# Sums of products in a Mamba block: accumulating DMAs in place of transposes and a vector add, under a new instruction order

## The chip, the cores and the metric

The kernel runs on one core of one Trainium2 chip. The time is the device time of one execution in microseconds; the time of a kernel is the median of its runs. The core has a matrix engine (TensorE, "PE" in the profile; its weight loads are "PEld"), a vector engine (VectorE, DVE), an activation engine (ScalarE, ACT), GpSimd (POOL), a queue engine that mostly issues transfers (SyncE, SP), and 16 DMA engines that all queues share.

## The reference, cut to what matters

One sequence of 4096 positions with 1024 features goes through half an FFN step, a Mamba block and another half FFN step, each behind a layer norm without weights:

```python
x = x + 0.5 * ffn(layernorm(x))      # weights rounded to -1, 0, 1 times a scale
x = x + mamba(layernorm(x))
x = x + 0.5 * ffn(layernorm(x))

# mamba
u, z = split(x @ W_in.T)             # 1024 features each
u = silu(conv(u, 4 taps) + conv_b)
dt_r, B, C = split(u @ W_xproj.T)    # 64, 16, 16
dt = softplus(dt_r @ W_dt.T + b_dt)
h_t = exp(dt * A) * h_(t-1) + dt * B_t * u_t      # 16 states for each feature
y_t = sum over the 16 states of h_t * C_t, + u * Dskip
out = (y * silu(z)) @ W_out.T
```

The sum over the states is what the change deals with: for every feature and position there are 17 terms, 16 products `h * C` and the skip `u * Dskip`.

## The kernel before, in words

All arithmetic is float32; the FFN splits its input in a high and a low part, so that two fast matmuls do for one.

**Tiling.** The sequence is cut into 16 chunks (`c`) of 256 positions, and the 1024 features of the Mamba block into two halves (`half`) of four blocks of 128 features. A half of a chunk is a tile of 128 partitions (features) by 4 x 256 elements, 512 KB. The recurrence runs over 32 halves, and in each over 16 states `n`.

**The recurrence of a state.** SP fetches rows B and C of the state, broadcast over the partitions (`bc`, six buffers, `fetch`). POOL writes `h = g * B` (line 934, `g = u * dt`) and adds what comes over from the chunk before to the first column (line 944); there are three `h` buffers. ACT makes the decays `da` (line 911) into PSUM. DVE scans `h` along the positions (line 969, two scans a state) and multiplies by C into a product `p` (line 985); there are five `p` buffers. ACT saves the last column (line 952) and the buffer of `h` comes free.

**The sum over the terms.** A term that is summed alone goes to PE: eight transposes of 128 x 128 (line 1052, `summed`) add it in PSUM to `y`, which also turns it from features by positions to positions by features. To save transposes, some pairs of terms are added first. Three states of each half (`SENT`: 1, 5 and 9) are sums by DMA: POOL issues an accumulating DMA that adds product `n - 1` onto product `n` within SBUF (line 1020, `beside`). One state of a middle chunk's half (`PAIRED`: 7), two of a half in the first chunk (12 and 14) and none in the last chunk are added by DVE (line 1002, `paired`). So a half in the middle has 13 terms left for PE out of 17. DVE then multiplies `y` by `silu(z)` (line 1069, `gate`), PE turns the result back (line 743) and multiplies by W_out (line 751).

**Around the recurrence**, the chunk before and the chunk after are worked on at the same time: statistics and norm (lines 382 to 401), transposes (417), the FFN (488, its residual on DVE in line 468), the projections to `u` (608) and `z` (668), convolution (539 on ACT, 549 on DVE). Weights stream from HBM through five buffers (lines 353, 360 and 366, issued by SP, loaded two or three blocks ahead). The FFN's bias is added to `x` by an accumulating DMA of POOL (line 461).

**What sets the order.** The program is written out by a planner that runs when the kernel is built (`Streams`). Every part is a generator that asks for an engine with a duration and an earliest time; the planner gives the engine to whichever can start first, by rank where several can, and holds an engine back for a better rank within `HOLD`. The constants at the top are its reckoning: `ISSUE` and `ADDED` for an accumulating DMA (600 and 9500 ns), `LATE_*` for what it adds to the end of an operation, ranks such as `SUM` and `RECUR`, and `TRIG`, which says after which step of the recurrence each part of the neighbouring chunks may start. The order that comes out is fixed on each engine: an instruction waits in its engine's queue, and what stands behind it waits too. The planner's times decide only this order; on the chip, semaphores do.

Of the kernel before, what the change touches and what calls it, by code (L numbers as in the profile page):

```python
# [27 lines left out]

FULL, PASS, TURN = 0.844, 0.449, 0.855
REACH = 160  # L30
ISSUE, ADDED = 600, 9500
SWITCH = 1300

LATE_P, LATE_X, LATE_D, LATE_N = 400, 100, 1700, 1300
PAIRED = (7,)
PAIRED_FIRST = (12, 14)
PAIRED_LAST = ()
TRIG = (-11, -16, 5, 1, -6, -16, 16, -2, 9, 12, 0, -17, 7, -7, -19, -8, -12)
ENTERED = 2
POOLED = ()  # L40
SENT = (1, 5, 9)
DEFER = 2.2, 3.2
Q_SOON = False

DECAY, ENTER, SUM, PREPARE, RECUR, GATE = 5, 0, 0, 0, 4, 1
FFN_A, NORM, U_PART, CONV, DELTA, OUT, FFN_C = 0, 5, 1, 3, 4, 2, 1

HOLD = (1300, 0, 100, 2600)
Z = (5, 7)


class Streams:
# [109 lines left out]
def macaron_mamba_kernel(  # L162
# [169 lines left out]

    def streamed(load, n, ahead, rank):

        queue = []

        def fill():
            for i in range(n):
                yield lambda: 0 if len(queue) < ahead else INF
                w = yield from weights.take()  # L340
                load(i, w)
                queue.append((order.now + 5000, w))

        order.spawn(fill(), rank)
        return queue

    def arrived(queue):
        yield lambda: queue[0][0] if queue else INF
        return queue.pop(0)[1]

    def u_weights(i, w):
# [76 lines left out]
            order.spawn(parts(g, pt, end + REACH), rank)  # L428


    def ffn(c, which, rank, at, tiles=range(TT)):
        ln, rows_, at = yield from stats(c, at, tiles)
        key = which, c

        def split(t):

            xn, begin = yield from normed(c, ln, rows_, t, at)
            hi = yield from his.take()
            lo = yield from los.take()
            ends = []  # L440

            def cut(g, pt, at_):
                part_hi, part_lo = (flat(p_[:, 4 * g : 4 * g + 4, :]) for p_ in (hi, lo))
                end = yield act(512, at_)
                nc.scalar.copy(part_hi, pt)  # L445
                end = yield dve(600, end + REACH)
                nc.vector.tensor_tensor(part_lo, pt, part_hi, ALU.subtract)  # L447
                banks.put(pt, end)
                ends.append(end)
                if len(ends) == NB // 4:  # L450
                    ready["parts", key, t] = end + REACH + LATE_N
                    parts[t] = lo, hi

            order.spawn(biased(t, begin), rank)
            yield from transposed(xn, begin, cut, rank)

        def biased(t, at_):

            yield from when("hbias")
            end = yield pool(ISSUE, at_, False)  # L460
            nc.gpsimd.dma_start(x_tiles[c, t], hbias.to_broadcast([P, D]), accum_op=ALU.add)
            ready["bias", key, t] = end + ADDED

        def residual(t, cols, pf, at_):
            at_ = max(at_, (yield from when("bias", key, t)))
            end = yield dve(660, at_)
            xt = x_tiles[c, t][:, cols]
            nc.vector.scalar_tensor_tensor(xt, pf, hscl, xt, ALU.mult, ALU.add)  # L468
            (ys if (*key, t) == ("a", 0, 1) else banks).put(pf, end)
            ready["ffn", key, t, cols.start] = end  # L470
            if key == ("c", NC - 1):
                yield from give_out(c, t, cols, end)

        parts = {}
        for t in tiles:
            order.spawn(split(t), rank)
        if key == ("a", 0):
            yield from as_weights_come(key, parts, residual, rank)
        for t in tiles if key != ("a", 0) else ():
            begin = yield from when("parts", key, t)  # L480
            lo, hi = parts[t]
            for h in range(2):
                cols = slice(h * OH, (h + 1) * OH)
                pf = yield from banks.take()
                for x in (lo, hi):
                    end = yield pe(8 * OH * PASS, 0, "r")
                    for k in range(NB):
                        nc.tensor.matmul(  # L488
                            pf,
                            x[:, k, :],  # L490
                            wf[:, k, cols],
                            start=(x is lo and k == 0),
                            stop=(x is hi and k == NB - 1),
                        )
                order.spawn(residual(t, cols, pf, end + REACH + LATE_X), rank)
            los.put(lo, end)
            his.put(hi, end)
        lns.put(ln, end if key != ("a", 0) else order.now)
        ends = {}
        for t in tiles:  # L500
            left = yield from when("ffn", key, t, 0)
            right = yield from when("ffn", key, t, OH)
            ends[t] = max(left, right)
        return ends

    def as_weights_come(key, parts, residual, rank):

        for t in range(TT):
            yield from when("parts", key, t)
        groups = {}  # L510
        for h in range(2):
            groups[0, h] = yield from banks.take()
            groups[1, h] = yield from ys.take()
        for k in range(NB):
            yield from when("wf", k)
            end = yield pe(8 * OH * PASS, 0, "r")
            for (t, h), pf in groups.items():
                for i in range(2):
                    nc.tensor.matmul(
                        pf,  # L520
                        parts[t][i][:, k, :],
                        wf[:, k, h * OH : (h + 1) * OH],
                        start=(k == 0 and i == 0),
                        stop=(k == NB - 1 and i == 1),
                    )
        for (t, h), pf in groups.items():
            order.spawn(residual(t, slice(h * OH, (h + 1) * OH), pf, end + REACH), rank)
        for t in range(TT):
            los.put(parts[t][0], end)
            his.put(parts[t][1], end)  # L530
# [4 lines left out]
    def conv(c, blk, pp, at):  # L535
        half, b = divmod(blk, HB)
        ub, rows_ = u[c, half][:, b, :], pp[:, KER - 1 : KER - 1 + T]
        end = yield act(T, at)
        nc.scalar.activation(  # L539
            ub,  # L540
            rows_,
            AF.Identity,
            bias=pr[:, blk, C_CB : C_CB + 1],
            scale=pr[:, blk, C_CW + KER - 1 : C_CW + KER],
        )
        for k in range(KER - 1):
            end = yield dve(391, end + (REACH if k == 0 else 111))
            tap = pr[:, blk, C_CW + k : C_CW + k + 1]
            nc.vector.scalar_tensor_tensor(ub, pp[:, k : k + T], tap, ub, ALU.mult, ALU.add)  # L549
        banks.put(pp, end)  # L550
        done = ready.setdefault(("conv", c, half), [])
        done.append(end)
        if len(done) == HB:
            end = yield act(D, end + REACH, "silu")
            nc.scalar.activation(flat(u[c, half]), flat(u[c, half]), AF.Silu)
            ready["u", c, half] = end + REACH

    def front():
        for c in range(NC):
# [28 lines left out]
            for t in range(TT):  # L588
                xn, at = xns[t]
                yield from transposed(xn, at, keep, NORM)  # L590
                while len(ends) < 2 * (t + 1):
                    yield lambda: ends[2 * t + 1] if len(ends) > 2 * t + 1 else INF

            end = yield pool(190)
            nc.gpsimd.tensor_copy(xT[:, :, PAD - KER + 1 : PAD], halo)  # L595
            at = max(end, ends[-1]) + REACH
            yield U_PART
            for blk in range(NB):
                yield from step(c, 2 + blk // 2)
                if blk % HB == 0:  # L600
                    u[c, blk // HB] = yield from us.take()
                pp = yield from banks.take()
                w = yield from arrived(queue)
                wt = w.rearrange("p (k m) -> p k m", m=P)
# [75 lines left out]
    def kept(c, half, b, pp, at):  # L680
        end = yield act(512, at)
        nc.scalar.copy(sz[c, half][:, :, b * P : (b + 2) * P], pp)
        banks.put(flat(pp), end)
        if b + 2 == HB:
            z = flat(sz[c, half])
            end = yield act(D, end + 125, "silu")
            nc.scalar.activation(z, z, AF.Silu)
            ready["z", c, half] = end + REACH

# [37 lines left out]
    def turned(c, half, yT):  # L727
# [15 lines left out]
                nc.tensor.transpose(pt[:, cols], sz[c, half][:, t, cols], ident)  # L743
            order.spawn(keep(t, pt, end + REACH), OUT)
        szs.put(sz[c, half], end)
        yield lambda: ends[-1] if len(ends) == TT else INF

    def by_w_out(po, yT, w, half, t):
        wt = w.rearrange("p (k m) -> p k m", m=QW)
# [207 lines left out]
    def recur():  # L957
        behind = None
        for c, half, n in items:
# [4 lines left out]
            for j in range(2):  # L964
# [3 lines left out]
                rows_ = flat(h[:, 2 * j : 2 * j + 2, :])  # L968
                nc.vector.tensor_tensor_scan(rows_, flat(da), rows_, 0.0, ALU.mult, ALU.add)  # L969
                decays.put(da, end)  # L970
                ready["step", (2 * c + half) * NST + n] = end
                if behind and j == 0:
                    yield from left(*behind)
                if behind and j == (0 if Q_SOON else 1):
# [38 lines left out]
    def beside(c, half, n):  # L1013
# [4 lines left out]
        if n in SENT:  # L1018
            end = yield pool(ISSUE, at, False)
            nc.gpsimd.dma_start(flat(p), flat(q), accum_op=ALU.add)  # L1020
            end = end + ADDED
        else:
            for j in range(0, HB, 2):
                end = yield pool(1250, at, True)
# [128 lines left out]
```

## Time and profile before

| | |
|---|---|
| median of 3 runs | 2602.99 us (2601.02 to 2603.2) |
| the profiled execution | 2601.62 us, span from first to last instruction 2599.9 us |
| busy PE, DVE, ACT, POOL | 2441.9, 2314.4, 1925.1, 1896.4 us |
| transposes of the sum on PE (line 1052) | 3328, 438.5 us |
| adds of pairs on DVE (line 1002) | 32, 53.7 us |
| sums by DMA (line 1020) | 96, issue 85.5 us on POOL in all |
| bytes moved by DMA | 461.03 MB, 177 GB/s |

In the rows of the profile, `L934` is line 934 of the kernel, `out<-in` the tiles that an instruction writes and reads, `x1024` how many there are; then come the busy time in all, the mean duration of one, the idle time of the engine just before, and what ended most of it. fp32 matmuls stand as two instructions each. "`A <- B`: total, times, longest" in the waits means that A stood still until B was done. The DMA share is the mean busy share of the 16 DMA engines.

### The profile page before, as it was taken

What the parts mean: (1) busy time and instruction counts of PE and PEld (TensorE: products, weight loads), DVE (VectorE), ACT (ScalarE), POOL (GpSimd) and SP (SyncE); (2) the same over time, 40 slices, a digit from 0 to 9 for tenths busy, and PEclk for the clock granted to TensorE, in tenths of its full rate; (3) what the DMA queues carried; (4) which work ended last, traced back from release to release, by engine and by line L of the source; (5) the groups of instructions that cost most, each with busy time, mean ns of one, the idle gap of its engine ahead of it and who ended that gap; (6) DMA issues with size and microseconds to landing.
All of it is one profiled execution on the core that took longest, in us unless ns stands there. A gap on an engine that the chain in (4) does not pass through costs nothing. (4 is left out here: it accounts for less than half of the span.)

```text
span 2599.9 us, 39031 instructions
## 1 busy us (share of the span) xinstructions
PE 2441.9 (94%) x13058; PEld 2093.8 (81%) x13058; DVE 2314.4 (89%) x2468; ACT 1925.1 (74%) x4056; POOL 1896.4 (73%) x2041
## 2 busy tenths in 40 slices
PE   5988899999999999999999999999999999999787
PEld 4776787888888888888888888888888888887676
DVE  4588998999999899999989999899999989999795
ACT  3678677687877868787786868878687786877563
POOL 0467867778787787878778686877878677787683
PEclk9989999999999999999999999999999999999888
DMA  4546556766766666666566765665675567666462
GB/s 165 156 129 187 175 158 178 198 180 195 197 173 166 196 185 199 186 182 188 167 190 195 203 178 161 189 195 168 196 207 168 167 193 191 188 192 173 149 165 65
DMA packets 232369, 461.03 MB, mean 177 GB/s; under 512 B 20708, under 2 KB 87396, under 8 KB 232168
## 3 DMA queue, kind: packets, MB, share of 16 engines
q1 hardware_dynamic: 209128, 374.65, 43.2%
q0 software_dynamic: 23040, 83.90, 18.6%
q8 instruction: 103, 1.69, 0.3%
q14 instruction: 98, 0.80, 0.1%
HBM read 390.82 MB, written 17.31 MB: 157 GB/s over the span
## 5 line engine op out<-in xcount | busy, mean ns | idle before, releaser
L934 POOL TENSOR_TENSOR h<-u,bc 128x512 f32<-128x512 f32 x1024 | 1339.5, 1335 | 444.9 <-ACT da L911 153.2
L969 DVE TENSOR_TENSOR_SCAN h<-da,h 128x512 f32<-128x512 f32 x1024 | 1215.4, 1206 | 78.8 <-ACT da L911 54.9
L911 ACT ACTIVATE da<-dt,pr 128x255 f32<-128x255 f32 x2048 | 953.1, 474 | 409.2 <-DVE h L969 373.7
L985 DVE TENSOR_TENSOR p<-h,bc 128x1024 f32<-128x1024 f32 x512 | 672.5, 1314 | 0.1
L1052 PE MATMUL y<-ident,p 128*128 128x128 f32 x3328 | 438.5, 278 | 69.0 <-DVE p L985 35.0
L668 PE MATMUL bank<-weight,xT 128*128 128x256 f32 x2048 | 479.5, 383 | 14.5 <-DMA weight<-in_w_in 9.6
L608 PE MATMUL bank<-xT,weight 128*128 128x259 f32 x2048 | 475.4, 385 | 14.3 <-POOL xT L595 5.2
L1052 PEld LDWEIGHTS y<-ident,p 128*128 128x128 f32 x3328 | 387.0, 143 | 124.1 <-DVE p L985 48.5
L751 PE MATMUL bank<-weight,u 128*128 128x256 f32 x2016 | 452.6, 381 | 7.7 <-DMA weight<-in_w_out 7.1
L608 PEld LDWEIGHTS bank<-xT,weight 128*128 128x128 f32 x2048 | 382.1, 191 | 77.3 <-issue 8.9
L668 PEld LDWEIGHTS bank<-weight,xT 128*128 128x128 f32 x2048 | 378.6, 192 | 65.9 <-ACT da L911 9.8
L751 PEld LDWEIGHTS bank<-weight,u 128*128 128x128 f32 x2016 | 381.4, 191 | 60.4 <-issue 5.6
L944 POOL TENSOR_TENSOR h<-h,over 128x4 f32<-128x4 f32 x512 | 272.0, 531 | 36.1
L488 PE MATMUL bank<-wf,lo 128*128 128x512 f32 x976 | 258.3, 407 | 5.3 <-DVE lo L447 3.8
L488 PE MATMUL bank<-wf,hi 128*128 128x512 f32 x976 | 243.3, 391 | 0.0
L488 PEld LDWEIGHTS bank<-wf,lo 128*128 128x128 f32 x976 | 181.5, 191 | 49.7 <-DVE x L468 7.6
L549 DVE SCALAR_TENSOR_TENSOR u<-bank,pr,u 128x256 f32<-128x256 f32 x384 | 176.8, 469 | 43.4 <-ACT u L539 40.9
L488 PEld LDWEIGHTS bank<-wf,hi 128*128 128x128 f32 x976 | 182.8, 189 | 37.6
L417 PE MATMUL bank<-ident,tmp 128*128 128x128 f32 x756 | 116.0, 288 | 38.1 <-ACT tmp L401 26.6
L386 ACT ACTIVATE tmp<-x,ln 128x1024 f32<-128x1024 f32 x96 | 110.1, 1146 | 37.8 <-POOL ln L384 37.6
L417 PEld LDWEIGHTS bank<-ident,tmp 128*128 128x128 f32 x756 | 95.5, 149 | 51.6 <-ACT tmp L401 28.8
L468 DVE SCALAR_TENSOR_TENSOR x<-bank,hscl,x 128x512 f32<-128x512 f32 x124 | 91.6, 739 | 43.4 <-PE bank L488 41.9
(99 smaller groups left out, 1936.2 us busy)
## 6 DMA issues: line engine op xcount, KB each, us to landing
bc<-bcd SPq DMA_DIRECT2D x512, 256.0 KB, 4.1
weight<-in_w_in SPq DMA_DIRECT2D x128, 512.0 KB, 4.8
weight<-in_w_in SPq DMA_DIRECT2D x256, 256.0 KB, 5.3
weight<-in_w_out SPq DMA_DIRECT2D x128, 512.0 KB, 6.1
p<-p POOLq DMA_DIRECT2D x96, 512.0 KB, 5.8
x<-hbias POOLq DMA_DIRECT2D x64, 512.0 KB, 8.1
x<-in_x SPq DMA_DIRECT2D x32, 512.0 KB, 4.7
out<-x SPq DMA_DIRECT2D x30, 512.0 KB, 4.7
```

Source lines behind the costliest of these rows:

```text
L417: nc.tensor.matmul(pt[:, j * P : (j + 1) * P], xn[:, k * P : (k + 1) * P], ident, start=(j == 0), stop=(j == 3), is_transpose=True, skip_g ...
L488: nc.tensor.matmul(pf, x[:, k, :], wf[:, k, cols], start=(x is lo and k == 0), stop=(x is hi and k == NB - 1),)
L549: nc.vector.scalar_tensor_tensor(ub, pp[:, k : k + T], tap, ub, ALU.mult, ALU.add)
L608: nc.tensor.matmul(pp[:, : KER - 1 + T], wt[:, k, :], xT[:, k, PAD - KER + 1 : PAD + T], start=(k == 0), stop=(k == NB - 1),)
L668: nc.tensor.matmul(pp[:, t, :], xT[:, k, PAD + t * P : PAD + (t + 1) * P], wt[:, :, i, :], start=(k == 0 and t == 0), stop=(k == NB - 1), ...
L751: nc.tensor.matmul(po[:, t, :], yT[:, b, t * P : (t + 1) * P], wt[:, b, :], start=(half == 0 and t == 0 and b == 0), stop=(half == 1 and b ...
L911: nc.scalar.activation(da[:, i, 1:], dt[c, half][:, b, 1:], AF.Exp, scale=a_neg[:, half * HB + b, n : n + 1],)
L934: nc.gpsimd.tensor_tensor(h[:, some, :], u[c, half][:, some, :], bc[:, 0:1, :].to_broadcast([P, ENTERED, T]), ALU.mult,)
L944: nc.gpsimd.tensor_tensor(h[:, :, 0], h[:, :, 0], over[c, half][:, :, n], ALU.add)
L969: nc.vector.tensor_tensor_scan(rows_, flat(da), rows_, 0.0, ALU.mult, ALU.add)
L985: nc.vector.tensor_tensor(p, h, bc[:, 1:2, :].to_broadcast([P, HB, T]), ALU.mult)
L1052: nc.tensor.matmul(y[t][:, b * P : (b + 1) * P], p[:, b, t * P : (t + 1) * P], ident, start=(first and b == 0), stop=(final and b == HB - ...
```

## The change

In every half the products of all even states (0, 2, ..., 14) get the term before them added by an accumulating DMA within SBUF, eight in place of three, and DVE adds no pair any more. So nine terms of 17 are left for PE: the eight sums and state 15. For the reckoning, such a sum ends 7500 ns after its issue (`SUMMED`); the bias of the FFN keeps 9500 (`ADDED`).

The planner's reckoning waits for each stage by name where it took the last of a list before (the cuts of the FFN's input, each block of the convolution, each part of `z`, both parts of a transposed tile), and `streamed` counts the weights that have been taken. `Silu` of the convolution becomes a stream of its own (`activated`). All ranks, holds, late times and triggers have new values, so that the order of the instructions on all engines is another. The computation is the same, and so is the number of every other operation.

```diff
-ISSUE, ADDED = 600, 9500
+ISSUE, ADDED, SUMMED = 600, 9500, 7500
-LATE_P, LATE_X, LATE_D, LATE_N = 400, 100, 1700, 1300
-PAIRED = (7,)
-PAIRED_FIRST = (12, 14)
+LATE_P, LATE_X, LATE_D, LATE_N = 700, 500, 0, 0
+PAIRED = ()
+PAIRED_FIRST = ()
 PAIRED_LAST = ()
-TRIG = (-11, -16, 5, 1, -6, -16, 16, -2, 9, 12, 0, -17, 7, -7, -19, -8, -12)
+TRIG = (-7, 5, -12, -40, -7, 0, 7, 22, 4, -4, -12, 1, 1, -3, -15, -40, 37)
-SENT = (1, 5, 9)
+SENT = (0, 2, 4, 6, 8, 10, 12, 14)
-DECAY, ENTER, SUM, PREPARE, RECUR, GATE = 5, 0, 0, 0, 4, 1
-FFN_A, NORM, U_PART, CONV, DELTA, OUT, FFN_C = 0, 5, 1, 3, 4, 2, 1
-HOLD = (1300, 0, 100, 2600)
-Z = (5, 7)
+DECAY, ENTER, SUM, PREPARE, RECUR, GATE = 6, 4, 4, 3, 9, 2
+FFN_A, NORM, U_PART, CONV, DELTA, OUT, FFN_C = 3, 3, 5, 4, 4, 6, 5
+HOLD = (5650, 0, 0, 0)
+Z = (9, 8)
...
     def streamed(load, n, ahead, rank):
-        queue = []
+        queue, gone = [], []
         def fill():
             for i in range(n):
-                yield lambda: 0 if len(queue) < ahead else INF
+                if i >= ahead:
+                    yield lambda: gone[i - ahead] if len(gone) > i - ahead else INF
                 w = yield from weights.take()
                 load(i, w)
                 queue.append((order.now + 5000, w))
...
+    def cuts(key, t):
+        for g in range(NB // 4):
+            yield from when("cut", key, t, g)
...
-                ends.append(end)
-                if len(ends) == NB // 4:
-                    ready["parts", key, t] = end + REACH + LATE_N
-                    parts[t] = lo, hi
+                ready["cut", key, t, g] = end + REACH + LATE_N
...
-        done = ready.setdefault(("conv", c, half), [])
-        done.append(end)
-        if len(done) == HB:
-            end = yield act(D, end + REACH, "silu")
-            nc.scalar.activation(flat(u[c, half]), flat(u[c, half]), AF.Silu)
-            ready["u", c, half] = end + REACH
+        ready["conv", c, blk] = end + REACH
+
+    def activated(c, half):
+        for blk in range(half * HB, (half + 1) * HB):
+            end = yield from when("conv", c, blk)
+        end = yield act(D, end, "silu")
+        nc.scalar.activation(flat(u[c, half]), flat(u[c, half]), AF.Silu)
+        ready["u", c, half] = end + REACH
...
-                while len(ends) < 2 * (t + 1):
-                    yield lambda: ends[2 * t + 1] if len(ends) > 2 * t + 1 else INF
+                yield lambda: max(ends) if len(ends) == NB // 4 * (t + 1) else INF
...
+        ready["kept", c, half, b] = end + 125
         if b + 2 == HB:
+            for b in range(0, HB, 2):
+                end = yield from when("kept", c, half, b)
             z = flat(sz[c, half])
-            end = yield act(D, end + 125, "silu")
+            end = yield act(D, end, "silu")
...
                 decays.put(da, end)
-                ready["step", (2 * c + half) * NST + n] = end
+                if j:
+                    ready["step", (2 * c + half) * NST + n] = end
...
             nc.gpsimd.dma_start(flat(p), flat(q), accum_op=ALU.add)
-            end = end + ADDED
+            end = end + SUMMED
```

More of the change, by code (lines that the diff above doesn't have):

```diff
@@ L344, in streamed @@
         order.spawn(fill(), rank)
-        return queue
+        return queue, gone
     def arrived(queue):
-        yield lambda: queue[0][0] if queue else INF
+        queue, gone = queue
+        at = yield lambda: queue[0][0] if queue else INF
+        gone.append(at)
         return queue.pop(0)[1]
@@ L439, in split @@
             lo = yield from los.take()
-            ends = []
+            parts[t] = lo, hi
             def cut(g, pt, at_):
@@ L479, in ffn @@
         for t in tiles if key != ("a", 0) else ():
-            begin = yield from when("parts", key, t)
+            yield from cuts(key, t)
             lo, hi = parts[t]
@@ L508, in as_weights_come @@
         for t in range(TT):
-            yield from when("parts", key, t)
+            yield from cuts(key, t)
         groups = {}
@@ L590, in front @@
                 yield from transposed(xn, at, keep, NORM)
-                while len(ends) < 2 * (t + 1):
-                    yield lambda: ends[2 * t + 1] if len(ends) > 2 * t + 1 else INF
+                yield lambda: max(ends) if len(ends) == NB // 4 * (t + 1) else INF
             end = yield pool(190)
             nc.gpsimd.tensor_copy(xT[:, :, PAD - KER + 1 : PAD], halo)
-            at = max(end, ends[-1]) + REACH
+            at = max(end, max(ends)) + REACH
             yield U_PART
@@ L601, in front @@
                     u[c, blk // HB] = yield from us.take()
+                    order.spawn(activated(c, blk // HB), CONV)
                 pp = yield from banks.take()
@@ L745, in turned @@
         szs.put(sz[c, half], end)
-        yield lambda: ends[-1] if len(ends) == TT else INF
+        yield lambda: max(ends) if len(ends) == TT else INF
     def by_w_out(po, yT, w, half, t):
```

## The prediction

> **What bounds the kernel now.** I read the page's busy line and DMA queues first, then the middle of the run by windows, then who waits for whom there, then the tile of the products.
>
> ```profile
> PE 2441.9 (94%) x13058; PEld 2093.8 (81%) x13058; DVE 2314.4 (89%) x2468; ACT 1925.1 (74%) x4056; POOL 1896.4 (73%) x2041
> ...
> PEclk9989999999999999999999999999999999999888
> ...
> q1 hardware_dynamic: 209128, 374.65, 43.2%
> q0 software_dynamic: 23040, 83.90, 18.6%
> ```
>
> PE is busiest and DVE five points behind; the clock is near full, so PE's time is work. DMA engines are busy for about 62%; q0 holds what POOL issues (96 sums of products, 64 additions of the bias).
>
> The kernel repeats itself by chunk. Two starts of the same instruction (timeline of POOL) give the period, 1234.62 - 1081.18 = 153.4 us:
>
> ```profile
> 1081.18 1.23 POOL L595 COPY xT<-halo 128x24 f32<-128x24 f32 x1
> ...
> 1234.62 1.23 POOL L595 COPY xT<-halo 128x24 f32<-128x24 f32 x1
> ```
>
> The windows view of 730 to 1690 us, 960 / 153.4 = 6.26 periods: length, then PE, PEld, DVE, ACT, POOL busy, clock, DMA share, GB/s. The second row counts only line 1052 (the transposes that sum on PE), the third only line 1002 (the adds of a pair on DVE).
>
> ```profile
> 730.00:1690.00 960.00, 936.62 (x5102) 806.59 (x5101) 888.63 (x947) 747.68 (x1581) 744.35 (x797) 1.00 0.65 184
> ...
> 730.00:1690.00 960.00, 165.74 (x1288) 146.49 (x1288) 1.00 0.65 184
> ...
> 730.00:1690.00 960.00, 21.18 (x13) 1.00 0.65 184
> ```
>
> In one period PE is busy for 936.62 / 6.26 = 149.7 us and idle for 3.7; DVE is busy for 142.0 and idle for 11.4. PE sets the period, DVE is close behind. Of DVE's idle time, the waits of DVE in the same window show what PE itself causes:
>
> ```profile
> DVE h L969 <- ACT da L911: 15.7, 7, 2.2
> DVE x L468 <- PE bank L488: 13.7, 13, 1.9
> DVE x L722 <- PE bank L751: 13.0, 7, 1.9
> DVE h L969 <- POOL h L944: 9.8, 12, 1.4
> ```
>
> The two PE rows make 26.7 us, 4.3 a period. The other 7.1 are waits for ACT and POOL, which a shorter PE does not cure. PE's waits over the whole span name two for transfers, 16.7 us in all:
>
> ```profile
> PE bank L668 <- DMA weight<-in_w_in: 9.6, 7, 4.5
> ...
> PE bank L751 <- DMA weight<-in_w_out: 7.1, 2, 5.4
> ```
>
> Last, the groups by line of the three operations that the change trades, and how long a sum by DMA takes from issue to landing (tile view of p):
>
> ```profile
> L1052 PE MATMUL y<-ident,p 128*128 128x128 f32 x3328 | 438.5, 278 | 69.0 <-DVE p L985 35.0 <-DVE p L1002 23.6 <-DVE sz L1069 10.3
> ...
> L1002 DVE TENSOR_TENSOR p<-p,p 128x1024 f32<-128x1024 f32 x32 | 53.7, 1678 | 0.0
> ```
>
> ```profile
> L1020 POOL DMA_DIRECT2D p<-p x96: 860/881/948, 119.0 to 2539.3; - x96
> ...
> DMA to landing us min/median/max: 4.6/5.8/10.7
> ```
>
> **The change, part by part.** *PE.* A half has 17 products (the skip and 16 states); each that is not folded into another costs PE 8 transposes. Before, three DMA sums and mostly one DVE add leave 13; after, eight DMA sums leave 9. The program of the changed kernel has 2304 transposes in place of 3328. At 438.5 / 3328 = 0.132 us of PE each, 1024 of them are 134.9 us. In the period (64 fewer at 165.74 / 1288 = 0.129) that is 8.2 us: PE goes from 149.7 to 141.5. The other matmuls are as many as before.
>
> *DVE.* The 32 adds of line 1002 go, 53.7 us; per period two at 21.18 / 13 = 1.63, 3.3 us: 142.0 becomes 138.7.
>
> *POOL.* 160 more issues at 0.88 us: ten a period, 8.8 us, so 118.9 (744.35 / 6.26) becomes 127.7. Each stands in order on POOL, and behind it the entry of the next state (line 934), for which DVE's scan waits. By then the product is there: before line 1020 POOL's idle time is mostly 0.2 to 0.3 us. Cover: POOL keeps some 20 us idle in a period of 148, and three h buffers let it run ahead. Without that cover ten issues would cost DVE 8.8 us a period, 132 us in all; I take zero.
>
> *DMA.* q0's 18.6% of 2599.9 us is 483.6 us of all 16 engines for 160 transfers, 3.02 us each. Ten more a period are 30.2 us on 0.65 x 153.4 = 99.7: 129.9 us, a share of 0.88 of a 148 us period in place of 0.65. It stays under PE's sum, so the transfers as such do not become the bound, but they queue. What that costs PE in late weights no row shows. Bounds: zero, if the weights come early enough, and 483 us, if each of the 160 added sums holds up a weight load that PE stands for by its whole 3.02 us; below nothing it can't go, since no transfer is taken away. I take the nearest row: PE waited 16.7 us for weights beside 160 software transfers; 160 more make it twice that, 17 us more, 1.1 a period.
>
> [...] The 16.7 us that PE in fact waited speak for most loads being early enough.
>
> *The summed product itself.* It reaches PE later than an unsummed one. The program lets PE's transposes follow 7.5 us after the issue (SUMMED; before, 9.5, ADDED), against a landing of 5.8 us in the middle and 10.7 at worst. PE works in order, so everything behind them on PE (projections, FFN blocks) waits if the sum is late. Both products of a pair also keep their buffers until the landing; there are five, DVE makes a product every 4.6 us (148 / 32), and the first of a pair is held for some 11 us (4.6 for its partner, 0.9 for the issue, 5.8 to land). Bounds: a gain of at most 58.6 us (35.0 + 23.6, PE's waits for products in the group row), and a loss of 1254 us, if each of 256 sums held PE for the 4.9 us between the median and the longest landing. I take zero, by the median, which lies under 7.5.
>
> *The new order* (TRIG, ranks, HOLD, LATE) and the waits of the reckoning for every named stage move instructions on all engines, the weight loads on SP's queue among them, and change no count. It can win back at most PE's idle 3.7 us a period (56 us in 15 periods); the loss is bounded only by what DVE's idle shows an order can cost, 11.4 a period (171 us). I take zero.
>
> **The sum.** By PE: 141.5 + 3.7 + 1.1 = 146.3 us a period. By DVE: 138.7 + 11.4 = 150.1 if all its idle time stays, 145.8 without what PE causes. With two engines this close each waits for the other, so I take the middle of 146.3 and 150.1: 148.2, 5.2 less than 153.4. Fifteen such periods lie between the first and last chunk's gates; start and end I leave as they are. 15 x 5.2 = 78, so the span goes from 2599.9 to 2521.9 us. The profiled execution took 2601.62, 1.7 more than its span, and the median, 2602.99, 1.4 more than that: 2525 us.
>
> **The rivals.**
> - *All of PE's relief shows* (13%): 2603 - 135 = 2468 us. For it: PE is busy for 97.6% of the middle, so its plan follows the bound closely. Against: DVE would have 138.7 us to do in 145.2 with ACT and POOL waits of 7.1, and more transfers.
> - *Late weights and crowded buffers eat most of it* (20%): 2560 to 2597. For it: a DMA share of 0.88. A mean of 0.2 us for each of 256 sums is 51 us off the 78: 2576. Against: PE's small waits for weights now.
> - *Sums land too late for PE's order, slower* (23%): at 0.88 the landing of a sum passes the 7.5 us that the order gives it, and PE stands before its transposes with everything queued behind. It decides from 78 / 256 = 0.30 us for each sum; at 0.5 us it is 128 - 78 = 50 us worse than before, 2653 us. For it: landings up to 10.7 us already at a share of 0.65. Against: the median leaves 1.7 us.
> - *The change doesn't do what it says*: the counts of the program exclude it.
>
> **How the numbers follow.** The forecast (2490 to 2560 us) has 42%, the full gain 13%, most of it eaten 20%; slower has 23%, and 2% is left for a time within 0.2%, which is about 5 us and about what a measurement of this kernel can tell. So faster 0.75, same 0.02, slower 0.23. The range runs from 2460, a little below the full gain, to 2640, just under the price of the slower case, and leaves out about 15%.
>
> **What would show it.** Right: PE's transposes at 304 us (2304 x 0.132), DVE's busy time near 2261, a period of 146 to 150, a DMA share of 0.85 to 0.9 in the middle, PE waiting 30 to 40 us for weights. Wrong on the slow side: PE waiting before line 1062 for DMA p, or landings of p above 7.5 us in the median. Wrong on the fast side: a period under 146, with DVE above 95%. If POOL's idle before line 943 falls and DVE's waits for h from POOL rise above 1.6 us a period, the issues on POOL were not free.

## The result, and the profile after

The changed kernel takes 2741.39 us (median of 4 runs, 2732.58 to 2748.42) against 2603.06: a ratio of 1.0532, 95% interval 1.0498 to 1.0565. It is 138 us slower where 78 less were forecast. The profiled execution took 2738.14 us with a span of 2736.4. Its page:

```profile
PE 2392.4 (87%) x12034; PEld 2023.2 (74%) x12034; DVE 2305.2 (84%) x2436; ACT 1927.4 (70%) x4059; POOL 1945.4 (71%) x2201
...
PEclk9998999999999999999999999999999999999988
...
q1 hardware_dynamic: 209128, 374.65, 42.3%
q0 software_dynamic: 46080, 167.79, 33.0%
...
L674 PE MATMUL bank<-weight,xT 128*128 128x256 f32 x2048 | 533.0, 412 | 167.8 <-DMA weight<-in_w_in 156.8
...
L1062 PE MATMUL y<-ident,p 128*128 128x128 f32 x2304 | 297.0, 276 | 38.1 <-DMA p<-p 38.0
```

PE is busy for 49.5 us less than before, although its transposes alone fell from 438.5 to 297.0; and it is idle for 2736.4 - 2392.4 = 344 us, where it was 158. The waits of PE name the idle time:

```profile
PE bank L674 <- DMA weight<-in_w_in: 156.8, 27, 9.8
PE bank L420 <- ACT tmp L404: 42.4, 17, 12.5
PE y L1062 <- DMA p<-p: 38.0, 20, 10.1
PE bank L614 <- ACT da L920: 16.9, 12, 1.4
...
PE bank L760 <- DMA weight<-in_w_out: 11.8, 4, 8.2
```

Before, the weights of `z` (line 668, now 674) cost PE 9.6 us. Two starts of one instruction of POOL, the same as in the prediction, give the period, 1281.69 - 1114.43 = 167.3 us, against 153.4:

```profile
1114.43 0.20 POOL L600 COPY xT<-halo 128x24 f32<-128x24 f32 x1
...
1281.69 0.20 POOL L600 COPY xT<-halo 128x24 f32<-128x24 f32 x1
```

One place of each period holds the loss: in each of the five periods from 776.2 to 1616 us PE waits 12.4 to 13.5 us for the weights of `z`, in two stalls, and the period grew by 13.9. These are the windows of 5 us around that place in the period above (columns as before: PE, PEld, DVE, ACT, POOL busy, clock, DMA share, GB/s):

```profile
1200.00:1205.00 5.00, 4.65 (x27) 3.96 (x26) 5.00 (x6) 4.84 (x11) 3.71 (x5) 1.00 0.71 202
1205.00:1210.00 5.00, 4.25 (x24) 3.50 (x22) 4.58 (x4) 2.68 (x8) 1.49 (x4) 1.00 0.91 290
1210.00:1215.00 5.00, 1.29 (x3) 1.14 (x4) 2.36 (x2) 4.51 (x10) 3.36 (x6) 0.74 1.04 301
1215.00:1220.00 5.00, 5.00 (x17) 4.07 (x17) 0.69 (x1) 2.67 (x7) 4.92 (x7) 0.58 1.11 321
1220.00:1225.00 5.00, 0.98 (x7) 0.64 (x5) 1.82 (x2) 2.27 (x5) 2.26 (x3) 1.00 1.08 249
1225.00:1230.00 5.00, 0.86 (x2) 0.81 (x3) 0.00 (x0) 0.00 (x0) 0.00 (x0) 0.60 0.88 256
1230.00:1235.00 5.00, 5.00 (x20) 4.07 (x20) 0.97 (x2) 1.44 (x3) 0.00 (x0) 0.71 0.00 0
```

For 25 us the DMA engines are full (share about 1), then they have nothing to do at all (0.00). While they are full, PE, DVE, ACT and POOL come to a stop one after another. What was issued then is in SP's timeline:

```profile
1204.13 0.33 SPq L224 DMA_DIRECT2D x<-in_x  x1
1204.55 0.38 SPq L772 DMA_DIRECT2D out<-x  x1
1205.03 1.81 SPq L363 DMA_DIRECT2D weight<-in_w_in  x2
1206.94 0.43 SPq L890 DMA_DIRECT2D bc<-bcd  x1
1207.46 3.58 SPq L369 DMA_DIRECT2D weight<-in_w_out  x3
1211.14 1.54 SPq L890 DMA_DIRECT2D bc<-bcd  x2
1212.79 23.15 SPq L363 DMA_DIRECT2D weight<-in_w_in  x6
```

The next chunk's `x`, a store, one block of `z`, three blocks of W_out, three rows of `bc`, and then the other blocks of `z`, which PE wants at once. POOL issued two sums (at 1205.08 and 1213.46) and two bias additions (1215.61 and 1216.50) beside them. A load of `z` takes up to 15.4 us here, against 5.5 in the median of the whole run.

### The profile page after: what moved, and what is told of

Same layout as the page of the kernel before. It is cut to its first block, busy times and chain, and to the rows that moved or that the text cites. A ratio compares the mean times of both kernels' runs of the same rounds, so it can differ in the third digit from the quotient of the medians.

```text
span 2736.4 us, 37306 instructions
## 1 busy us (share of the span) xinstructions
PE 2392.4 (87%) x12034; PEld 2023.2 (74%) x12034; DVE 2305.2 (84%) x2436; ACT 1927.4 (70%) x4059; POOL 1945.4 (71%) x2201
## 5 line engine op out<-in xcount | busy, mean ns | idle before, releaser
L995 DVE TENSOR_TENSOR p<-h,bc 128x1024 f32<-128x1024 f32 x512 | 721.0, 1408 | 10.3 <-PE y L1062 10.1
L674 PE MATMUL bank<-weight,xT 128*128 128x256 f32 x2048 | 533.0, 412 | 167.8 <-DMA weight<-in_w_in 156.8
L674 PEld LDWEIGHTS bank<-weight,xT 128*128 128x128 f32 x2048 | 414.7, 208 | 241.9 <-DMA weight<-in_w_in 90.2
L760 PE MATMUL bank<-weight,u 128*128 128x256 f32 x2016 | 459.7, 382 | 12.0 <-DMA weight<-in_w_out 11.8
L1062 PE MATMUL y<-ident,p 128*128 128x128 f32 x2304 | 297.0, 276 | 38.1 <-DMA p<-p 38.0
L1062 PEld LDWEIGHTS y<-ident,p 128*128 128x128 f32 x2304 | 267.6, 143 | 65.1 <-DMA p<-p 18.3
L1030 POOL DMA_DIRECT2D p<-p x256 | 227.1, 887 | 73.3 <-DVE p L995 49.2
L953 POOL TENSOR_TENSOR h<-h,over 128x4 f32<-128x4 f32 x512 | 251.8, 492 | 30.2
L492 PE MATMUL bank<-wf,lo 128*128 128x512 f32 x976 | 253.7, 403 | 17.2 <-ACT xd L646 13.9
L454 DVE TENSOR_TENSOR lo<-bank,hi 128x512 fp32r<-128x512 f32 x125 | 83.4, 687 | 204.4 <-ACT hi L452 204.4
L492 PEld LDWEIGHTS bank<-wf,lo 128*128 128x128 f32 x976 | 181.8, 190 | 67.1 <-ACT xd L646 16.7
L420 PE MATMUL bank<-ident,tmp 128*128 128x128 f32 x756 | 127.5, 303 | 57.8 <-ACT tmp L404 42.4
L452 ACT CAST hi<-bank 128x512 fp32r<-128x512 f32 x125 | 70.0, 583 | 147.7 <-PE bank L420 147.3
```

Source lines behind the costliest of these rows:

```text
L492: nc.tensor.matmul(pf, x[:, k, :], wf[:, k, cols], start=(x is lo and k == 0), stop=(x is hi and k == NB - 1),)
L674: nc.tensor.matmul(pp[:, t, :], xT[:, k, PAD + t * P : PAD + (t + 1) * P], wt[:, :, i, :], start=(k == 0 and t == 0), stop=(k == NB - 1), ...
L760: nc.tensor.matmul(po[:, t, :], yT[:, b, t * P : (t + 1) * P], wt[:, b, :], start=(half == 0 and t == 0 and b == 0), stop=(half == 1 and b ...
L953: nc.gpsimd.tensor_tensor(h[:, :, 0], h[:, :, 0], over[c, half][:, :, n], ALU.add)
L995: nc.vector.tensor_tensor(p, h, bc[:, 1:2, :].to_broadcast([P, HB, T]), ALU.mult)
L1062: nc.tensor.matmul(y[t][:, b * P : (b + 1) * P], p[:, b, t * P : (t + 1) * P], ident, start=(first and b == 0), stop=(final and b == HB - ...
```

## The experiments

Two theories. L: the transfers of the sums fill the DMA engines and make the weights late. O: the new order by itself makes them late, with or without the sums.

**1. The sums cut to slivers, same order** (`a_sliver_sums`), and **the old sums in the new order, the new sums in the old one, the reckoning alone.** A kernel with slivers issues and waits as before, and leaves most of each sum out of its result. The diffs put several constants on one line.

```diff
# a_sliver_sums, against the changed kernel
-            nc.gpsimd.dma_start(flat(p), flat(q), accum_op=ALU.add)
+            nc.gpsimd.dma_start(p[:, 0, 0:8], q[:, 0, 0:8], accum_op=ALU.add)
# b_sums_old_order, against the kernel before
-SENT = (1, 5, 9); PAIRED = (7,); PAIRED_FIRST = (12, 14)
+SENT = (0, 2, 4, 6, 8, 10, 12, 14); PAIRED = (); PAIRED_FIRST = (); SUMMED = 7500
# c_order_old_sums, against the changed kernel
-SENT = (0, 2, 4, 6, 8, 10, 12, 14); PAIRED = (); PAIRED_FIRST = ()
+SENT = (1, 5, 9); PAIRED = (7,); PAIRED_FIRST = (12, 14)    # reckoned with ADDED
# d_reckoning_alone, against the changed kernel
+all constants and sums of the kernel before
```

> The changed kernel with the same instructions in the same order, but each of the 256 sums by DMA moves 8 columns in place of 1024, so most of the sum is left out of the result; issues and waits stay. Theory L (the sums' transfers, 30 us of all DMA engines in each period, are what makes the weights late): the stall of PE before the z projection (line 674, 157 us for DMA in the changed kernel) falls under 30 us, the period goes from 168 to about 148 us and the time to some 2480 us. Theory O (the new order bunches the loads of x, z, W_out and the stores in one stretch of SP's queue, and that alone makes them late): the stall stays above 100 us and the time above 2650 us.

> The kernel before with all its constants and its reckoning, but with the eight sums by DMA in each half, none on DVE, a sum reckoned to land after 7.5 us. Theory L: the same 256 transfers meet the old order's loads, PE waits more than 100 us for weights and the time is above 2650 us. Theory O: PE waits for weights under 50 us and the time falls below 2603 us, to 2500 to 2560 us.

> The changed kernel with its new constants and reckoning, but with the old sums: three by DMA in each half (reckoned 9.5 us), one on DVE (two in the first chunk, none in the last). Theory L: with 96 transfers in place of 256 PE's wait for z weights falls under 40 us; PE has 135 us more to do, so the time is about 2600 us. Theory O: the wait stays, the z stall is above 100 us and the time is above 2700 us.

> The changed kernel's reckoning (waits for named stages) with all constants and sums of the kernel before. Both theories: the reckoning alone matters little, within 1% of before, 2580 to 2630 us. If it costs over 2% it is a part of the loss by itself.

Measured: a 2580.20 us (ratio to before 0.9918, 0.9903 to 0.9933), b 2664.67 (1.0241, 1.0224 to 1.0259), c 2664.74 (1.024, 1.0224 to 1.0255), d 2710.37 (1.0417, 1.0402 to 1.0433). The waits of PE in a:

```profile
PE bank L420 <- ACT tmp L404: 69.5, 29, 12.4
PE bank L674 <- DMA weight<-in_w_in: 32.2, 22, 4.0
PE y L1062 <- DMA p<-p: 19.4, 4, 8.0
```

Nothing but the bytes of the sums differs between a and the changed kernel, and they are worth 161 us: the wait for `z` falls from 156.8 to 32.2. That is theory L, although a does not reach the 2480 us that it named. The mechanism of theory O does not show: in c, with the old sums, PE waits only 9.4 us for `z`. Yet c is 62 us above before. Its waits of PE lie elsewhere:

```profile
PE bank L420 <- ACT tmp L404: 72.1, 30, 12.5
PE bank L420 <- DVE lo L454: 39.5, 32, 2.7
...
PE bank L674 <- DMA weight<-in_w_in: 9.4, 6, 5.7
```

b fits neither theory whole: PE waits 44.5 us for `z`, under O's 50, and the time is L's. The path from before to after runs 2603, +62 for order and reckoning (c), -85 from c to a (the work that the sums spare, and another order), +161 for the bytes of the sums. d says that the reckoning with the old constants costs 108 us, which neither theory expected.

**2. How the load hurts.** The sliver again in the old order; half of every sum; the loads of `z` cut; the loads of W_out cut.

```diff
# f_sliver_old_order, against b: the sliver of a
# g_half_sums, against the changed kernel
+            nc.gpsimd.dma_start(p[:, 0:2, :], q[:, 0:2, :], accum_op=ALU.add)
# k_sliver_z, against the changed kernel
-                w[:, j], w_in[NB + 2 * pair + j][:, part_ * HB : (part_ + 1) * HB, :]
+                w[:, j, 0, 0:8], w_in[NB + 2 * pair + j][:, part_ * HB, 0:8]
# l_sliver_out, against the changed kernel
-            w.rearrange("p (k m) -> p k m", m=QW),
-            w_out[:, half * HB : (half + 1) * HB, q * QW : (q + 1) * QW],
+            w.rearrange("p (k m) -> p k m", m=QW)[:, 0, 0:8],
+            w_out[:, half * HB, q * QW : q * QW + 8],
```

> The kernel of b_sums_old_order (eight sums a half, old constants and reckoning), with each sum cut to 8 columns, so most of the sum is left out. Theory T (the instructions saved bring what was forecast and the transfers' load takes it away, in either order): the time falls from 2665 to some 2520 us, as the sliver brought 161 us under the new order. Theory O (the load matters only where the new order bunches its loads): it falls by under 60 us, to above 2600 us.

> The changed kernel, same order, each sum by DMA over half of its columns (512 of 1024), the rest of the sum left out. Between the sliver (2580 us) and the whole (2741 us). If the loss grows evenly with the load: about 2660 us. If it is a threshold, because transfers queue only once the engines are full for long: well under 2640 us, and PE's wait for z weights nearer to the sliver's 32 us than to 157 us.

> The changed kernel, same order, all sums whole, but the loads of the z weights cut to 8 columns of each block, so that z is computed from old contents of the buffers. If late z weights are what the sums' load costs: PE's stall before line 674 vanishes and the time falls to about 2580 us, the sliver's. If the landing of the sums themselves costs as much: PE still waits for p in line 1062, and the time stays above 2650 us.

> The changed kernel, same order, all sums whole, but the loads of W_out cut to 8 columns of one row block, so that the output projection uses old contents. In k_sliver_z the small loads of z were as late as the whole ones, so it would be their place in the queue, behind the three blocks of W_out and the x and bc rows issued just ahead, that makes them late while the sums slow everything down. If so: PE's stall before line 674 falls from 157 us to under 50 us and the time to some 2600 us. If it is the bc rows, the stores or the sums alone: the stall stays above 100 us and the time above 2680 us.

Measured: f 2628.54 us (1.0105, 1.0087 to 1.0124), g 2660.71 (1.0227, 1.0205 to 1.0248), k 2716.71 (1.0437, 1.0417 to 1.0457), l 2609.67 (1.0026, 1.0016 to 1.0036).

Half a sum costs half: g lies 81 us under the changed kernel and 81 above a. No threshold shows between these three points. In the old order the same bytes cost 36 us (b less f), under the 60 of theory O in that expectation, so what a transfer costs depends on what it meets. And f, which spares the same work and moves almost no bytes for its sums, is still 27 us slower than the kernel before: what its order and the added issues on POOL cost is more than that work brings.

k and l tell what the transfers meet. Both take about 66 MB of loads away (q1 moves 308.6 and 308.1 MB in place of 374.7). Of the time of all 16 engines that is 160 us in k and 210 in l, by q1's share of the span. But k wins 25 us, l 132. The waits of PE, first in k, then in l:

```profile
PE bank L674 <- DMA weight<-in_w_in: 137.1, 23, 10.8
PE bank L420 <- ACT tmp L404: 47.2, 23, 12.5
PE y L1062 <- DMA p<-p: 39.3, 21, 8.4
```

```profile
PE bank L674 <- DMA weight<-in_w_in: 59.2, 15, 6.1
PE bank L420 <- ACT tmp L404: 44.1, 17, 12.8
PE y L1062 <- DMA p<-p: 36.6, 21, 9.6
```

The time of the loads of `z` from issue to landing, in the changed kernel, in k and in l:

```profile
DMA to landing us min/median/max: 2.7/5.5/16.0
DMA to landing us min/median/max: 1.5/4.5/16.1
DMA to landing us min/median/max: 2.6/5.0/10.9
```

At worst a load of `z` of 4 KB is as late as one of 256 KB. So it is not its own bytes that are slow but what goes out in front of it, the loads of W_out above all. Whether these hold it up by their place in the queue or by their bytes, l cannot tell.

**3. One queue, or the bytes.** The same bytes issued by another engine, all orders on PE, DVE and POOL kept. The profile lists the loads that ACT issues as a queue of their own (q10, 67.1 MB).

```diff
# h_out_on_act, against the changed kernel; h_before_act the same against the kernel before
-        nc.sync.dma_start(                 # in out_weights
+        nc.scalar.dma_start(
# h_z_on_act, against the changed kernel
-            nc.sync.dma_start(             # in z_weights
+            nc.scalar.dma_start(
```

> The changed kernel with everything whole and PE, DVE and POOL in the same order, but the 128 loads of W_out issued on ACT's queue in place of SP's; the bytes are the same. If z is late because its loads stand behind W_out in one queue: PE's stall before line 674 falls from 157 to under 60 us and the time to some 2600 to 2640 us. If it is the bytes that the DMA engines have to move in that stretch, whatever the queue: the stall stays above 110 us and the time above 2690 us. ACT waits at each load for a free buffer, which can cost some of the gain.

> The kernel before with its 128 loads of W_out issued on ACT's queue, same order of the other engines: the control for h_out_on_act. PE waits there only 17 us for weights, so nothing to win: 2595 to 2620 us, slower if ACT's waits at the loads hold up its decays.

> The changed kernel with the z loads, the late ones, on ACT's queue, so that nothing of SP's stands in front of them; W_out stays on SP's. With W_out on ACT's the stall before line 674 was 103 us and the time 2669 us. If what was left there is x, bc and stores still ahead of z in SP's queue: the stall falls under 50 us and the time to some 2620 us. If it is the DMA engines' work itself: the stall stays near 100 us and the time near 2670 us. ACT's wait for a free buffer at each z load counts against it.

Measured: h_out_on_act 2669.18 us (1.0254, 1.0239 to 1.0269), h_before_act 2607.33 (1.0023, 1.0011 to 1.0036), h_z_on_act 2674.94 (1.027, 1.0249 to 1.0291). Moving W_out wins 72 us of the changed kernel and nothing of the kernel before. The loads of `z` do not go out earlier for it. In the period that follows 1092.61 us of h_out_on_act, the two blocks that PE stands for are issued 0.9 and 9.5 us after the load of `x` (at 1183.26 and 1191.88, `x` at 1182.36); in the changed kernel it is 0.9 and 8.7 (1205.03, 1212.79, 1204.13). The waits of PE in h_out_on_act and in h_z_on_act:

```profile
PE bank L674 <- DMA weight<-in_w_in: 102.9, 20, 9.2
```

```profile
PE bank L420 <- ACT tmp L404: 124.1, 30, 12.6
PE y L1062 <- DMA p<-p: 59.0, 29, 8.2
...
PE bank L674 <- DMA weight<-in_w_in: 8.3, 3, 6.0
```

In h_out_on_act the wait for `z` lies between the two values of the expectation, and the DMA share of the windows of 5 us in that period still reaches 1.08. With `z` on a queue of its own its wait is gone (8.3 us) and its slowest load takes 10.1 us, yet the time is no better: now PE waits for the norm of ACT and for the sums. Of the norm's delay the trace names one part: ACT stands 62.2 us for the loads of `x`, 43.5 in the changed kernel. Whether the loads that ACT issues hold its norm up as well was not tested. So another queue wins back 66 to 72 us of the 161; the rest turned into other waits, and how much of it is ACT's holding and how much the engines' bytes these runs do not separate. Issuing the loads of W_out from ACT saved 72 us with the same bytes, and in the period looked at the late loads were issued no earlier.

**4. What an order is worth.** The kernel before with one number nudged, twice; the eight sums under two more settings.

```diff
# n_nudged, against the kernel before: LATE_P 400 -> 450
# t_before_x150, against the kernel before: LATE_X 100 -> 150
# t_sums_x150, against b: LATE_X 100 -> 150
# e_sums_reckoning, against d: the eight sums, SUMMED = 7500
```

> The kernel before with one number of the reckoning nudged, LATE_P from 400 to 450 ns; no operation is added or removed, the planner gives another order. If the order before is one picked from many and any other costs some per cent: 2640 to 2720 us, like the reckoning alone (2710 us). If not: within 1% of 2602 us.

> The kernel before with LATE_X 150 in place of 100 ns, nothing else: a second nudge. If the kernel before has an order picked from many: 2640 to 2720 us like LATE_P 450 (2694 us). If that one was bad luck: within 1% of 2602 us.

> b_sums_old_order (eight sums, old reckoning) with the same nudge, LATE_X 150 ns. To be set against t_before_x150. If untuned orders of eight sums scatter as those of the old sums do: 2640 to 2700 us, and under t_before_x150 by up to 80 us if the sums pay on level terms; above it if the transfers' load outweighs them.

> Eight sums a half under the old constants and the changed reckoning, to be compared with d_reckoning_alone (2710 us; same constants and reckoning, old sums), neither of which has constants fitted to it. If the eight sums save what was forecast once no side has a picked order: some 2630 us, 80 us under d. If their transfers eat it: 2690 to 2730 us, no better than d.

Measured: n_nudged 2694.32 us (1.0357, 1.0341 to 1.0373), t_before_x150 2666.94 (1.0246, 1.0227 to 1.0264), t_sums_x150 2727.09 (1.0475, 1.0458 to 1.0492), e 2806.89 (1.0787, 1.0769 to 1.0806). Fifty nanoseconds in one constant cost 64 and 93 us; no operation was added. The kernel before has an order that four others (n, t_before, c, d) with the same operations miss by 62 to 108 us. Set side by side, each row with the same constants and reckoning:

| constants, reckoning | old sums | eight sums | difference |
|---|---|---|---|
| old, old | 2602.1 | 2664.7 | +62.6 |
| LATE_X 150, old | 2666.9 | 2727.1 | +60.2 |
| old, changed | 2710.4 | 2806.9 | +96.5 |
| new, changed | 2664.7 | 2741.4 | +76.7 |

The kernel with eight sums is slower by 60 to 97 us in all four. Each difference also holds what the planner makes of the other order, so its size is not the price of the sums alone. e and t_sums_x150 came out slower than either side of their expectations.

**5. Can the order mend it?**

```diff
# h_ahead1, against the changed kernel
-                    queue = streamed(lambda i, w: out_weights(i // 2, i % 2, w), NB, 3, OUT)
+                    queue = streamed(lambda i, w: out_weights(i // 2, i % 2, w), NB, 1, OUT)
# m_arrive_8000, against the changed kernel
-                queue.append((order.now + 5000, w))
+                queue.append((order.now + 8000, w))
```

> The changed kernel with W_out loaded one block ahead in place of three; the planner gives another order. If the bunch of three W_out blocks in front of z is what costs: PE's stall before line 674 falls under 60 us and the time to 2600 to 2660 us, unless W_out itself is then late (line 760 waiting over 50 us). If not: above 2700 us.

> The changed kernel with the planner told that a streamed weight arrives 8000 ns after its issue in place of 5000, nearer to what the loads take beside the sums; another order. If the planner only lacked the true latency: PE's waits for weights fall under 60 us and the time under 2650 us. If the order is as good as any other untuned one: 2680 to 2780 us.

Measured: h_ahead1 2699.63 us (1.0373, 1.035 to 1.0397), m 2715.83 (1.0441, 1.0424 to 1.0459). In both, the wait for `z` falls as intended and others grow: in h_ahead1 it is 54.8 us, but PE waits 57.9 for sums (38.0 in the changed kernel) and 29.0 for W_out (11.8). PE's waits in m:

```profile
PE y L1062 <- DMA p<-p: 78.2, 22, 10.5
PE bank L674 <- DMA weight<-in_w_in: 64.9, 15, 7.8
PE bank L420 <- ACT tmp L404: 50.8, 14, 12.6
```

So neither single change finds an order in which the sums pay. No version with the whole computation beats the kernel before.

## Why the prediction was wrong

- **The counts held, the relief is open.** There are 2304 transposes (297.0 us, forecast 304), 256 sums and no add on DVE. What that saves was not isolated. From c to a the time falls by 85 us, where 78 was forecast; from the kernel before to f, also without the bytes of the sums, it rises by 27. The planner orders both sides of each pair differently, so the agreement of 85 with 78 may be luck.
- **The step that failed is the term for late weights.** The sum took 17 us for it, by doubling 16.7 us of waits beside 160 software transfers. Measured, PE waits 168.6 us for weights (156.8 + 11.8), 152 more than before. Whole sums against slivers cost 161 us, 0.63 for each of the 256. No run cuts the 160 added ones alone; at that price they are 101 us, an estimate, inside the stated bounds of 0 and 483. The 16.7 us were the result of one order, and the order was about to change: a nudge with the old sums (t_before_x150) already has 32.2 us of waits for `z` where the kernel before has 9.6.
- **The mean share hid the bunch.** The share was forecast at 0.88 and came out at 0.78 (410 to 2330 us), because the period grew and because 3.02 us was a mean over sums and bias additions: the 160 added transfers took 2.62 us of all engines each (33.0% of 2736.4 us less 18.6% of 2599.9, over 160). The windows of 5 us go from 1.11 to 0.00: the engines were late for 25 us and idle later. A mean under 1 does not say that loads arrive in time.
- **The new order at zero was the second miss.** With the old sums, order and reckoning together are worth +62 us (c), within the stated 171. The prediction read PE's 97.6% as a property of the kernel; it was the property of one order: from 410 to 2330 us PE is busy for 97.6% before and for 94.1 to 95.4% in c, d, n_nudged and t_before_x150, which do the same work.
- **The rivals.** "Late weights eat most of it" named the mechanism, with 0.2 us a sum where it was 161 / 256 = 0.63. The slower rival had the right sign and the wrong place: PE waits 38.0 us for sums, and the median landing, 6.4 us, stays under the order's 7.5.
- **PE's other work did not stay as it was.** Line 674 takes 533.0 us where 668 took 479.5, for the same 2048 instructions. The timeline of PE in the bunch shows why:

```profile
1205.64 3.62 PE L674 MATMUL bank<-weight,xT 128*128 128x256 f32 x16
1213.71 3.75 PE L674 MATMUL bank<-weight,xT 128*128 128x256 f32 x8 [4.46 <-DMA weight<-in_w_in]
...
1229.14 3.75 PE L674 MATMUL bank<-weight,xT 128*128 128x256 f32 x8 [8.15 <-DMA weight<-in_w_in]
1232.68 0.69 PE L420 MATMUL bank<-ident,tmp 128*128 128x128 f32 x4
1233.21 1.89 PE L674 MATMUL bank<-weight,xT 128*128 128x256 f32 x8
```

After each of these two stalls, 4.46 and 8.15 us long, eight matmuls take 3.75 us, twice the 1.89 of the eight at 1233.21, and the granted clock in those windows is 0.58 to 0.74. The same 3.75 us follow each of the ten stalls for `z` from 776.2 to 1616 us, which last 4.38 to 8.64 us. In all, PE is busy for 2392.4 us, 46 more than with the slivers (2346.0) in the same order, 40 of them in line 674 (493.3 there): a stall is paid a second time in slow matmuls.
- **POOL's issues.** In the window of 730 to 1690 us DVE's waits for `h` from POOL fell from 9.8 to 6.4 us, 1.1 a period where more than 1.6 was the sign of "not free"; so taking zero stands. DVE's busy time fell by 9 us and not by 53.7: the product (line 985, now 995) takes 1408 ns in the mean where it took 1314. The slivers have 1401, so it is not the bytes; why, was not tried.

## What to carry to other kernels

Price added transfers by what they meet, not by the mean share of the DMA engines: look at windows of a few us for the stretch where loads bunch, and ask which load behind them is needed first. In a static order, small waits of the kernel before are no price list for a change that reorders everything; run the old order nudged by something harmless first, to learn how much any other order costs. To judge an idea apart from that, compare both versions under the same, equally unfitted settings.

## What the runs showed of the hardware that was not expected

- In the queue of one issuing engine a tiny load can be as late as a large one: loads of 4 KB landed after 16.1 us at worst, those of 256 KB after 16.0, and PE waited 137.1 us for the former, 156.8 for the latter. Issuing what stood in front of them (W_out) from another engine won 72 us with the same bytes.
- In one order the cost of the accumulating transfers grew evenly with their size, 81 us for each half; in another order the whole was less than a quarter of that (36 us against 161).
- The mean granted clock was 0.981 before, 0.976 with the slivers, and 0.952 in the changed kernel, whose periods of 167 us hold two stalls such as those of 4.46 and 8.15 us.
